# Two attention steps per turn, stages dealt out by turns, and row-wise work by pairs of row tiles, in a graph network with attention

## The chip, the core and the metric

The kernel runs on one core of one Trainium2 chip. The metric is device time in microseconds (us). In the profiles PE is TensorE's matmuls, PEld its weight loads, DVE VectorE, ACT ScalarE, POOL GpSimd, SP the engine that issues DMAs.

## The reference, cut to what matters

Layer 0 is a graph convolution with two batch norms, and the change does not touch it except for the last load. Layer 1, for each of 16 batches of 1024 rows and 256 columns, in four heads of 64:

```python
x = _layernorm(x + layer0(x, ...))
# layer 1
c_adj = mean of each row of x;  diff = c_adj[:, None, :] - c_adj[:, :, None]
Wg = adj * 2*abs(abs(sigmoid(diff) - 0.5) - 0.5)      # 1024 x 1024 per batch, symmetrised
q  = relu(fea @ Wg * para)                             # "graph"
k, v = x @ kv_w
out = softmax(q k^T * scale) v                         # 4 heads
x = _layernorm(x + out)
```

All of it is in fp32.

## The kernel before

For batch b the kernel needs four kinds of work: the attention of b itself; for b+1 the matrix Wg (`wg_a`, `wg_b`), the keys, the values and the queries (`graph`); for b+2 the row-wise work (`bn2`, `ln1_a`, `ln1_b`, `x1_t`, the means and their row `crow`). The finish (division by the softmax's sums, residual, layer norm, store) of b runs partly in b+1. The attention of a batch is cut into 16 steps; a step has 4 fp32 matmuls of scores, 2 exponentials of 128x1024, 2 sums and 4 matmuls of attend. All other work is cut into *pieces*, and a list says in which step each piece is issued:

```python
def put(w, s, f, *a):
    at.setdefault(w * NS + s, []).append((f, a))
# ... for each batch b (cut)
    for j in range(NT):                          # 8 row tiles, one per step
        put(b - 2, 4 + j, bn2, b, j)
        put(b - 2, 5 + j, ln1_a, b, j)
        put(b - 2, 7 + j, ln1_b, b, j)
        put(b - 2, 8 + j, x1_t, b, j)
    put(b - 2, 7 + NT, crow, b)
    # wg: one row tile per step; keys, values: steps 0 to 4; graph: steps 6 to 15 (cut)

for g in ...:
    scores(g + 1); exps(g + 1)                   # one step ahead
    sums(g)
    for f, a in at.get(g, []):
        f(*a)                                    # the pieces of this step
    attend(g)
```

So TensorE issues, per step: scores, pieces, attend. Every other engine gets its instructions in the same order of steps. (In the traces an fp32 matmul shows as two records and a transpose as one, so the four matmuls of scores are `x8`.) The row of means reads its input right behind the work that makes it:

```python
def crow(b):
    nc.vector.tensor_scalar_mul(css[b], css[b], 1.0 / C)     # DVE: the means
    # ... (cut)
    for h in range(NH):
        p = ps_t.tile([P, FB], F32, tag="t", name="pc")
        for k in range(FB // P):                              # TensorE needs them at once
            nc.tensor.transpose(p[:, ts(k, P)], css[b][:, j : j + 1].to_broadcast([P, P]), ident)
        nc.scalar.copy(crows[b][:, ts(h, FB)], p)
```

The matmuls come in forms: scores use 64 rows of the array, two heads side by side; attend uses 64 columns, two heads side by side; the sums of the softmax (`dens`) use 32 columns; everything else uses the full 128x128. In PSUM, the memory that TensorE writes to, stand two tiles of scores (two banks each), one of attend and three for the pieces.

## Time and profile before

| | before |
|---|---|
| time, median of the runs at first | 2781.89 us |
| span of the profile | 2780.6 us |
| period of a batch in the attention | 114.92 us |
| busy per period: PE, DVE, ACT, POOL | 113.7, 73.8, 65.2, 31.4 us |

The table is read thus: PE is busy nearly the whole period, every other engine has over 40 us to spare, so only TensorE's own issue, or something that it waits for, can move the end. The lines for this are in the prediction below. Two more groups, of DVE's row-wise work on one tile of 256 columns (columns: line, engine, operation, tiles, shapes, count; then busy us in total and mean ns of one; then idle time before them and who ended it):

```profile
L564 DVE TENSOR_TENSOR r<-r,x 128x256 f32<-128x256 f32 x128 | 54.4, 425 | 4.4
L557 DVE RECIPROCAL RD<-pf 128x4 f32<-128x4 f32 x128 | 23.1, 180 | 144.4 <-PE pf L555 144.4
```

They are short and many, and none of them makes TensorE wait.

### The profile page before, as it was taken

How to read it: one execution, taken by the hardware profiler on the slowest of the kernel's cores; microseconds unless marked ns; L12 is line 12 of the kernel's file. 1: busy time of each engine (PE TensorE's matmuls, PEld its weight loads, DVE VectorE, ACT ScalarE, POOL GpSimd, SP SyncE). 2: the span in 40 equal slices, each digit the busy share in tenths (PEclk: the TensorE clock that was granted, in tenths of full speed). 3: DMA queues.
4: the chain of work that ended last, by engine and by line, in shares of the span. 5: the costliest groups of instructions: out<-in, count | busy, mean ns of one | idle time of the engine just before them, and what ended most of it. 6: DMA issues, size and time to landing. Idle time of an engine off the chain costs nothing.

```text
span 2780.6 us, 26036 instructions
## 1 busy us (share of the span) xinstructions
PE 2724.5 (98%) x9306; PEld 1145.7 (41%) x9306; DVE 1353.0 (49%) x2377; ACT 1297.7 (47%) x1887; POOL 498.1 (18%) x660
## 2 busy tenths in 40 slices
PE   8999999999999899999999999999999999999998
PEld 4444444444444443443434434344343443444432
DVE  3101111112222655756657566575665756657556
ACT  2111111112655564655646546466465564655534
POOL 0000000000000212313223132231322313323113
PEclk9999999999999899999999999999999999999999
DMA  3212211210772200101101001010010100101000
GB/s 121 82 62 84 91 61 76 91 76 0 252 281 90 74 15 16 42 18 33 35 12 42 23 27 35 14 42 25 23 35 14 42 27 22 34 14 42 10 8 24
DMA packets 109992, 147.01 MB, mean 53 GB/s; under 512 B 10272, under 2 KB 92704, under 8 KB 103712
## 3 DMA queue, kind: packets, MB, share of 16 engines
q1 hardware_dynamic: 109856, 145.27, 15.2%
q8 instruction: 76, 1.25, 0.2%
q14 instruction: 60, 0.49, 0.1%
HBM read 86.52 MB, written 58.72 MB: 52 GB/s over the span
## 4 chain that ended last, share of the span: by engine, by line
PE 97%; DVE 2%; DMA 0%; issue 0%; POOL 0%; ACT 0%; SPq 0%; DVEq 0%; POOLq 0%; ACTq 0%
PE s L494 18%; PE o L524 17%; PE pg L474 16%; PE pa L215 16%; PE po L304 8%; PE ph L228 8%; PE pk L447 4%; PE pv L458 4%; PE pf L554 2%; PE pd L543 1%; PE py L387 1%; PE px L408 1%; PE pc L421 1%; PE pf L555 0%; DVE qT L479 0%
## 5 line engine op out<-in xcount | busy, mean ns | idle before, releaser
L506 ACT ACTIVATE e<-s 128x1024 f32<-128x1024 f32 x512 | 496.4, 1021 | 409.4 <-PE s L494 408.9
L494 PE MATMUL s<-qT,kT 64*128 64x512 f32 x2048 | 508.8, 615 | 0.0
L524 PE MATMUL o<-e,v 128*64 128x512 f32 x2048 | 495.7, 605 | 0.0
L515 DVE TENSOR_TENSOR acc<-acc,e 128x1024 f32<-128x1024 f32 x384 | 467.0, 1216 | 41.9 <-ACT e L506 27.5
L474 PE MATMUL pg<-wg,x 128*128 128x512 f32 x1024 | 477.1, 604 | 0.5 <-ACT x1T L409 0.2
L215 PE MATMUL pa<-AhT,x 128*128 128x512 f32 x1024 | 443.7, 594 | 0.5 <-issue 0.5
L247 DVE BATCH_NORM_STATS2 st<-ph 128x6 f32<-128x512 f32 x128 | 89.5, 699 | 560.1 <-ACT hT L246 560.1
L494 PEld LDWEIGHTS s<-qT,kT 64*128 64x128 f32 x2048 | 176.2, 186 | 327.0 <-issue 244.8
L215 PEld LDWEIGHTS pa<-AhT,x 128*128 128x128 f32 x1024 | 195.1, 191 | 246.3 <-issue 244.3
L474 PEld LDWEIGHTS pg<-wg,x 128*128 128x128 f32 x1024 | 182.2, 190 | 240.6 <-issue 213.4
L439 DVE SCALAR_TENSOR_TENSOR wg<-wg,adj_sb 128x1024 f32<-128x1024 f32 x128 | 156.7, 1225 | 171.9 <-ACT wg L435 169.6
L222 ACT COPY agg<-pa 128x512 f32<-128x512 f32 x64 | 37.5, 585 | 407.4 <-PE pa L215 407.4
L228 PE MATMUL ph<-agg,W1T 128*128 128x512 f32 x512 | 222.2, 592 | 0.0
L524 PEld LDWEIGHTS o<-e,v 128*64 128x64 f32 x2048 | 124.2, 136 | 225.5 <-issue 212.6
L66 POOL TENSOR_SCALAR rs_z<-mv_z 128x1 f32<-128x1 f32 x128 | 52.2, 408 | 900.3 <-DVE mv_z L343 889.3
L66 POOL TENSOR_SCALAR rs_a<-mv_a 128x1 f32<-128x1 f32 x128 | 124.8, 975 | 436.3 <-DVE mv_a L343 436.2
L304 PE MATMUL po<-hL,W2T 128*128 128x512 f32 x384 | 165.0, 592 | 0.0
L68 POOL TENSOR_TENSOR rs_a<-rs_a,mhalf 128x1 f32<-128x1 f32 x128 | 157.9, 1234 | 10.7
L409 ACT COPY x1T<-px 128x256 f32<-128x256 f32 x128 | 47.6, 372 | 240.4 <-PE px L408 240.4
L66 POOL TENSOR_SCALAR rs_bn<-mv_bn 128x1 f32<-128x1 f32 x6 | 1.3, 222 | 884.0 <-DVE mv_bn L104 884.0
L228 PEld LDWEIGHTS ph<-agg,W1T 128*128 128x128 f32 x512 | 97.3, 190 | 122.5 <-issue 122.2
L246 ACT COPY hT<-ph 128x512 f32<-128x512 f32 x128 | 74.9, 585 | 144.9 <-PE ph L228 144.9
(106 smaller groups left out, 2486.0 us busy)
## 6 DMA issues: line engine op xcount, KB each, us to landing
h<-hT SPq DMA_DIRECT2D x24, 1024.0 KB, 3.8
hL<-h SPq DMA_DIRECT2D x24, 1024.0 KB, 6.2
x<-in_x_dram SPq DMA_DIRECT2D x16, 1024.0 KB, 5.3
yT<-y SPq DMA_DIRECT2D x32, 512.0 KB, 3.7
yt<-yT SPq DMA_DIRECT2D x128, 128.0 KB, 2.6
xr<-in_x_dram SPq DMA_DIRECT2D x128, 128.0 KB, 2.3
out_dram<-r SPq DMA_DIRECT2D x128, 128.0 KB, 1.7
A<-in_adj_dram SPq DMA_DIRECT2D x4, 1024.0 KB, 7.9
```

What stands on the lines that cost most here:

```text
L66: nc.gpsimd.tensor_scalar(dst, src, add, None, op0=OP.add)
L68: nc.gpsimd.tensor_tensor(dst, src, mhalf[:, :n], OP.pow)
L215: nc.tensor.matmul(p, xts[b][:, k, ts(c, P)], AhT[:, k, ts(h, FB)], start=(k == 0), stop=(k == NT - 1),)
L228: nc.tensor.matmul(p, W1T[:, k, ts(f, P)], aggT[b][:, k, ts(h, FB)], start=(k == 0), stop=(k == CT - 1),)
L304: nc.tensor.matmul(po[c], W2T[:, k, ts(c, P)], hT[u][:, k, :], start=(k == 0), stop=(k == HT - 1))
L439: nc.vector.scalar_tensor_tensor(t, t, 1.0, adj_sb[:, i, :], op0=OP.add, op1=OP.mult)
L447: nc.tensor.matmul(p, kvw[:, k, ts(c, P)], x1Ts[b][:, k, ts(h, FB)], start=(k == 0), stop=(k == CT - 1))
L474: nc.tensor.matmul(pg[b], x1s[b, k][:, ts(c, P)], wgs[b, k][:, ts(h, FB)], start=(k == 0), stop=(k == NT - 1))
L494: nc.tensor.matmul(t[:, h, :], kTs[b, pair][h * HD : (h + 1) * HD, ts(cb, P)], qTs[b, pair][h * HD : (h + 1) * HD, ts(hf, FB)], start=True ...
L506: nc.scalar.activation(E[g, a], S.pop((g, a)), AF.Exp)
L515: nc.vector.tensor_add(ACC[b, hf, pair], ACC[b, hf, pair], E[g, a])
L524: nc.tensor.matmul(O[b, hf, pair][h * HD : (h + 1) * HD, :], vs[b][:, cb, pair * P + h * HD : pair * P + (h + 1) * HD], E[g, a][:, h, :], ...
```

## The change

The intent: fewer changes of the array's form on TensorE (two steps share one turn: scores, pieces, scores, attend, attend), half as many row-wise instructions (two row tiles at once), the means computed a turn ahead of their use, and within a turn the short pieces spread among the long ones, so that their PSUM tiles are evacuated in time. The core of the diff; most buffers, the loads and the general path are cut, and the comments are added:

```diff
-        def crow(b):
-
+        def means(b):
             nc.vector.tensor_scalar_mul(css[b], css[b], 1.0 / C)
...
-        def finish_a(b, i):
-            hf, k = divmod(i, FB // P)
+        def recips(b, hf):                       # one reciprocal for four row tiles
...
+        def finish_a(b, j):                      # two row tiles: one multiply, one add of 512 columns
...
-        ep = pool("ep", 5)
-        accp = pool("accp", 3)
+        ep = pool("ep", 6)
+        accp = pool("accp", 2)
...
         NS = NT // 2 * NP * NH
+        NC = NS // 2                             # 8 turns of two steps
...
+        WG = (3, 3, 1, 1)                        # wg stages in turns 0 to 3
+        KV = (3, 3, 2)                           # keys and values in turns 0 to 2
+        QG = (6, 6, 6, 7, 7)                     # graph pieces in turns 3 to 7
...
+            put(b - 2, NC - 2, means, b)
+            for h in range(NH):
+                put(b - 2, NC - 1, crow, b, h)
...
+        def arrange(pieces):
+            few = sorted((fa for fa in pieces if fa[0] not in long), key=lambda fa: rank.get(fa[0], 11))
+            many = [fa for fa in pieces if fa[0] in long]      # keys, values, graph
+            n = sum(f in short for f, _ in few)
+            res, k, done = [], 0, 0
+            for f, a in few:
+                res.append((f, a))
+                if f in short and f is not dens:
+                    k += 1
+                    upto = len(many) * k // n
+                    res += many[done:upto]
+                    done = upto
+            return res + many[done:]
...
+            scores(g + 2); exps(g + 2)           # (conditions cut)
+            sums(g)
+            for f, a in now:                     # arranged pieces of the turn
                 f(*a)
-            if 0 <= g < nsteps:
-                attend(g)
+            sums(g + 1)
+            scores(g + 3); exps(g + 3)
+            for k in live:                       # g and g + 1
+                attend(k)
```

In `rank` the functions `bn2` and, last of all, `wg_a` and `wg_b` come after the short pieces.

More of the change, by code (lines that the diff above doesn't have):

```diff
@@ L79, in gnn_norm_attention_kernel @@
     yT_dram = [yT_all[b] for b in range(B)]
-    LDP = 3
+    LDP = 2
     s2 = const.tile([P, CT], F32, name="s2")
@@ L273, in load @@
         def load(b, j):
-            yts[b, j] = ldp.tile([P, CT, P], F32, tag="yt", name=f"yt{b}_{j}")
-            nc.sync.dma_start(yts[b, j], yT_dram[b][:, :, ts(j, P)])
-            xrs[b, j] = ldp.tile([P, C], F32, tag="xr", name=f"xr{b}_{j}")
-            nc.sync.dma_start(xrs[b, j], x[b, ts(j, P), :])
+            yts[b, j] = ldp.tile([P, CT, 2 * P], F32, tag="yt", name=f"yt{b}_{j}")
+            nc.sync.dma_start(yts[b, j], yT_dram[b][:, :, ts(j, 2 * P)])
+            xrs[b, j] = ldp.tile([P, 2, C], F32, tag="xr", name=f"xr{b}_{j}")
+            nc.sync.dma_start(xrs[b, j], x[b, ts(j, 2 * P), :].rearrange("(a p) c -> p a c", p=P))
         with ExitStack() as ph2:
@@ L338, in ln_stats, with ln_apply @@
     def ln_stats(sm, r, name):
-        st = sm.tile([P, 6], F32, tag="st", name=f"st_{name}")
-        nc.vector.bn_stats(st, r)
-        mv = sm.tile([P, 2], F32, tag="mv", name=f"mv_{name}")
-        nc.vector.bn_aggr(mv, st)
-        rs = sm.tile([P, 1], F32, tag="rs", name=f"rs_{name}")
-        rsqrt(rs, mv[:, 1:2], EPS)
+        n = r.shape[1]
+        mv = sm.tile([P, n, 2], F32, tag="mv", name=f"mv_{name}")
+        for a in range(n):
+            st = sm.tile([P, 6], F32, tag="st", bufs=2, name=f"st_{name}_{a}")
+            nc.vector.bn_stats(st, r[:, a, :])
+            nc.vector.bn_aggr(mv[:, a, :], st)
+        rs = sm.tile([P, n], F32, tag="rs", name=f"rs_{name}")
+        rsqrt(rs, mv[:, :, 1], EPS)
         return mv, rs
-    def ln_apply(dst, r, mv, rs):
-        nc.vector.tensor_scalar(dst, r, mv[:, 0:1], rs, op0=OP.subtract, op1=OP.mult)
+    def ln_apply(r, mv, rs):
+        nc.vector.tensor_scalar(r, r, mv[:, 0, 0:1], rs, op0=OP.subtract, op1=OP.mult)
     def fast():
@@ L353, in fast @@
         pool = lambda name, bufs, **k: fx.enter_context(tc.tile_pool(name=name, bufs=bufs, **k))
-        x1p = pool("x1p", 21)
+        x1p = pool("x1p", 11)
         x1Tp = pool("x1Tp", 1)
@@ L358, in fast @@
         kp = pool("kp", 2 * CT)
-        qp = pool("qp", CT + 1)
+        qp = pool("qp", 2 * CT + 1)
         vp = pool("vp", 2)
-        ep = pool("ep", 5)
-        accp = pool("accp", 3)
+        ep = pool("ep", 6)
+        accp = pool("accp", 2)
         otp = pool("otp", 3)
         sm = pool("sm", 6)
-        rp = pool("rp", 4)
+        rp = pool("rp", 2)
         ps_s = pool("ps_s", 2, space=PSUM)
@@ L381, in begin @@
             x1Ts[b] = x1Tp.tile([P, CT, N], F32, tag="x1T", name=f"x1T_{b}")
-            css[b] = sm.tile([P, NT], F32, tag="cs", name=f"cs_{b}")
+            css[b] = sm.tile([P, NT], F32, tag="cs", bufs=2, name=f"cs_{b}")
         def ln1_a(b, j):
-            p = ps_t.tile([P, FB], F32, tag="t", name="py")
-            for c in range(CT):
-                nc.tensor.transpose(p[:, ts(c, P)], yts[b, j][:, c, :], ident)
-            x1s[b, j] = x1p.tile([P, C], F32, tag="x1", name=f"x1_{b}_{j}")
@@ L389, in ln1_a @@
-            nc.vector.tensor_add(x1s[b, j], p[:, :C], xrs[b, j])
+            p = ps_t.tile([P, 2, C], F32, tag="t", name="py")
+            for a in range(2):
+                for c in range(CT):
+                    nc.tensor.transpose(p[:, a, ts(c, P)], yts[b, j][:, c, ts(a, P)], ident)
+            x1s[b, j] = x1p.tile([P, 2, C], F32, tag="x1", name=f"x1_{b}_{j}")
+            nc.vector.tensor_add(x1s[b, j], p, xrs[b, j])
             mvs[b, j] = ln_stats(sm, x1s[b, j], f"a{b}_{j}")
         def ln1_b(b, j):
-            r = x1s[b, j]
@@ L394, in ln1_b @@
             mv, rs = mvs.pop((b, j))
-            nc.vector.scalar_tensor_tensor(
-                r,
-                r,
-                mv[:, 0:1],
-                rs.to_broadcast([P, C]),
-                op0=OP.subtract,
-                op1=OP.mult,
-                accum_out=css[b][:, j : j + 1],
-            )
-        def x1_t(b, j):
-            p = ps_t.tile([P, FB], F32, tag="t", name="px")
-            for c in range(CT):
-                nc.tensor.transpose(p[:, ts(c, P)], x1s[b, j][:, ts(c, P)], ident)
-            nc.scalar.copy(x1Ts[b][:, :, ts(j, P)], p[:, :C].rearrange("p (c n) -> p c n", c=CT))
@@ L411, in crow @@
-        def crow(b):
+            for a in range(2):
+                r = x1s[b, j][:, a, :]
+                nc.vector.scalar_tensor_tensor(
+                    r,
+                    r,
+                    mv[:, a, 0:1],
+                    rs[:, a : a + 1].to_broadcast([P, C]),
+                    op0=OP.subtract,
+                    op1=OP.mult,
+                    accum_out=css[b][:, 2 * j + a : 2 * j + a + 1],
+                )
+        def x1_t(b, j):
+            p = ps_t.tile([P, CT, 2 * P], F32, tag="t", name="px")
+            for a in range(2):
+                for c in range(CT):
+                    nc.tensor.transpose(p[:, c, ts(a, P)], x1s[b, j][:, a, ts(c, P)], ident)
+            nc.scalar.copy(x1Ts[b][:, :, ts(j, 2 * P)], p)
@@ L413, in crow @@
+        def means(b):
             nc.vector.tensor_scalar_mul(css[b], css[b], 1.0 / C)
-            hcs[b] = sm.tile([P, NT], F32, tag="hcs", name=f"hcs_{b}")
+            hcs[b] = sm.tile([P, NT], F32, tag="hcs", bufs=2, name=f"hcs_{b}")
             nc.vector.tensor_scalar_mul(hcs[b], css[b], 0.5)
-            crows[b] = crp.tile([P, N], F32, tag="crow", name=f"crow_{b}")
-            for h in range(NH):
-                p = ps_t.tile([P, FB], F32, tag="t", name="pc")
-                for k in range(FB // P):
-                    j = h * (FB // P) + k
-                    nc.tensor.transpose(p[:, ts(k, P)], css[b][:, j : j + 1].to_broadcast([P, P]), ident)
-                nc.scalar.copy(crows[b][:, ts(h, FB)], p)
+        def crow(b, h):
+            if h == 0:
+                crows[b] = crp.tile([P, N], F32, tag="crow", name=f"crow_{b}")
+            p = ps_t.tile([P, FB], F32, tag="t", name="pc")
+            for k in range(FB // P):
+                j = h * (FB // P) + k
+                nc.tensor.transpose(p[:, ts(k, P)], css[b][:, j : j + 1].to_broadcast([P, P]), ident)
+            nc.scalar.copy(crows[b][:, ts(h, FB)], p)
@@ L471, in graph @@
                 pg[b] = ps_t.tile([P, FB], F32, tag="t", name="pg")
-                if h == 0:
-                    qTs[b, c] = qp.tile([P, N], F32, tag="qT", name=f"qT_{b}_{c}")
+                qTs[b, c, h] = qp.tile([P, FB], F32, tag="qT", name=f"qT_{b}_{c}_{h}")
             nc.tensor.matmul(
-                pg[b], x1s[b, k][:, ts(c, P)], wgs[b, k][:, ts(h, FB)], start=(k == 0), stop=(k == NT - 1)
+                pg[b], x1s[b, k // 2][:, k % 2, ts(c, P)], wgs[b, k][:, ts(h, FB)], start=(k == 0), stop=(k == NT - 1)
             )
             if k == NT - 1:
-                qs = qTs[b, c][:, ts(h, FB)]
+                qs = qTs[b, c, h]
                 nc.vector.tensor_mul(qs, pg[b], para_sb[:, c, ts(h, FB)])
@@ L496, in scores @@
                         kTs[b, pair][h * HD : (h + 1) * HD, ts(cb, P)],
-                        qTs[b, pair][h * HD : (h + 1) * HD, ts(hf, FB)],
+                        qTs[b, pair, hf][h * HD : (h + 1) * HD, :],
                         start=True,
@@ L548, in fast @@
         R = {}
-        def finish_a(b, i):
-            hf, k = divmod(i, FB // P)
-            p = ps_t.tile([P, FB], F32, tag="t", name="pf")
-            for pair in range(NP):
-                nc.tensor.transpose(p[:, ts(pair, P)], OT[b, hf, pair][:, ts(k, P)], ident)
-            nc.tensor.transpose(p[:, C : C + P], DT[b, hf][:, ts(k, P)], ident)
-            rd = RD[:, b * NT + i, :]
-            nc.vector.reciprocal(rd, p[:, C : C + P].rearrange("p (h r) -> p h r", r=32)[:, :, 0])
-            r = rp.tile([P, C], F32, tag="r", name=f"r_{b}_{i}")
+        KB = FB // P
@@ new lines, in recips @@
+        def recips(b, hf):
+            p = ps_t.tile([P, KB, P], F32, tag="t", name="pr")
+            for k in range(KB):
+                nc.tensor.transpose(p[:, k, :], DT[b, hf][:, ts(k, P)], ident)
+            i = b * NT + hf * KB
+            nc.vector.reciprocal(
+                RD[:, i : i + KB, :], p.rearrange("p k (h r) -> p k h r", r=32)[:, :, :, 0]
+            )
+        def finish_a(b, j):
+            hf, k = divmod(2 * j, KB)
+            p = ps_t.tile([P, 2, C], F32, tag="t", name="pf")
+            for a in range(2):
+                for pair in range(NP):
+                    nc.tensor.transpose(p[:, a, ts(pair, P)], OT[b, hf, pair][:, ts(k + a, P)], ident)
+            r = rp.tile([P, 2, C], F32, tag="r", name=f"r_{b}_{j}")
+            rd = RD[:, b * NT + 2 * j : b * NT + 2 * j + 2, :].rearrange("p a h -> p (a h)")
@@ L559, in finish_a @@
             nc.vector.tensor_mul(
-                r.rearrange("p (h d) -> p h d", h=HEADS),
-                p[:, :C].rearrange("p (h d) -> p h d", h=HEADS),
-                rd.unsqueeze(2).to_broadcast([P, HEADS, HD]),
-            )
-            nc.vector.tensor_add(r, r, x1s.pop((b, i)))
-            mv, rs = ln_stats(sm, r, f"z{b}_{i}")
-            nm = sm.tile([P, 1], F32, tag="nm", name=f"nm_{b}_{i}")
-            nc.gpsimd.tensor_scalar(nm, mv[:, 0:1], rs, -1.0, op0=OP.mult, op1=OP.mult)
@@ L568, in finish_a @@
-            R[b, i] = (r, rs, nm)
-        def finish_b(b, i):
-            r, rs, nm = R.pop((b, i))
-            nc.scalar.activation(r, r, AF.Identity, bias=nm, scale=rs)
-            nc.sync.dma_start(out[b, ts(i, P), :], r)
+                r.rearrange("p a (h d) -> p (a h) d", h=HEADS),
+                p.rearrange("p a (h d) -> p (a h) d", h=HEADS),
+                rd.unsqueeze(2).to_broadcast([P, 2 * HEADS, HD]),
+            )
+            nc.vector.tensor_add(r, r, x1s.pop((b, j)))
+            mv, rs = ln_stats(sm, r, f"z{b}_{j}")
@@ new lines, in finish_a, with finish_b @@
+            nm = sm.tile([P, 2], F32, tag="nm", name=f"nm_{b}_{j}")
+            for a in range(2):
+                nc.gpsimd.tensor_scalar(
+                    nm[:, a : a + 1], mv[:, a, 0:1], rs[:, a : a + 1], -1.0, op0=OP.mult, op1=OP.mult
+                )
+            R[b, j] = (r, rs, nm)
+        def finish_b(b, j):
+            r, rs, nm = R.pop((b, j))
+            for a in range(2):
+                nc.scalar.activation(
+                    r[:, a, :], r[:, a, :], AF.Identity, bias=nm[:, a : a + 1], scale=rs[:, a : a + 1]
+                )
+            nc.sync.dma_start(out[b, ts(j, 2 * P), :].rearrange("(a p) c -> p a c", p=P), r)
@@ L603, in fast, with put @@
         NS = NT // 2 * NP * NH
+        NC = NS // 2
         at = {}
-        def put(w, s, f, *a):
-            at.setdefault(w * NS + s, []).append((f, a))
-        for b in range(B):
-            put(b - 2, 4, begin, b)
-            for j in range(NT):
-                if b > 0 or j >= LDP:
-                    put(b - 2, 3 + j, load, b, j)
-                put(b - 2, 4 + j, bn2, b, j)
-                put(b - 2, 5 + j, ln1_a, b, j)
-                put(b - 2, 7 + j, ln1_b, b, j)
-                put(b - 2, 8 + j, x1_t, b, j)
-            put(b - 2, 7 + NT, crow, b)
-            for i in range(NT):
-                put(b - 2, 8 + NT + i, wg_a, b, i)
-                put(b - 2, 8 + NT + i, wg_b, b, i)
-            n = 0
+        def put(w, t, f, *a):
+            at.setdefault(w * NC + t, []).append((f, a))
@@ new lines, in fast @@
+        WG = (3, 3, 1, 1)
+        KV = (3, 3, 2)
+        QG = (6, 6, 6, 7, 7)
+        for b in range(B):
+            for hf in range(NH):
+                t = (hf + 1) * (NC // NH)
+                put(b, t, dens, b, hf)
+                put(b, t + 1, recips, b, hf)
+                for k in range(KB // 2):
+                    put(b, t + 1 + k, finish_a, b, hf * (KB // 2) + k)
+                    put(b, t + 2 + k, finish_b, b, hf * (KB // 2) + k)
+            put(b - 2, 2, begin, b)
+            for j in range(NT // 2):
+                if b > 0 or j >= LDP:
+                    put(b - 2, j, load, b, j)
+                put(b - 2, j + 1, bn2, b, j)
+                put(b - 2, j + 2, ln1_a, b, j)
+                put(b - 2, j + 3, ln1_b, b, j)
+                put(b - 2, j + 4, x1_t, b, j)
+            put(b - 2, NC - 2, means, b)
+            for h in range(NH):
+                put(b - 2, NC - 1, crow, b, h)
+            i = 0
+            for t, n in enumerate(WG):
+                for i in range(i, i + n):
+                    put(b - 1, t, wg_a, b, i)
+                    put(b - 1, t, wg_b, b, i)
+                i += 1
@@ L625, in fast @@
             kv = [(keys, (b, c, h)) for c in range(CT) for h in range(NH)]
             kv += [(values, (b, j)) for j in range(0, NT, 2)]
-            for n, (f, a) in enumerate(kv):
-                put(b - 1, n * 5 // len(kv), f, *a)
-            ng = CT * NH * NT
-            for m in range(ng):
-                put(b - 1, 6 + m * 10 // ng, graph, b, m)
-            for i in range(NT):
-                hf = i // (FB // P)
-                s = (hf + 1) * (NS // NH)
-                if i % (FB // P) == 0:
-                    put(b, s, dens, b, hf)
-                put(b, s + 1 + i % (FB // P), finish_a, b, i)
-                put(b, s + 2 + i % (FB // P) + (b == B - 1 and hf == NH - 1), finish_b, b, i)
@@ L640, in fast @@
-        put(B - 1, NS // NH, range_so_far)
-        put(B - 1, NS + FB // P, range_all)
-        nsteps = B * NS
-        for g in range(min(at), max(max(at), nsteps - 1) + 1):
-            if 0 <= g + 1 < nsteps:
-                scores(g + 1)
-                exps(g + 1)
-            if 0 <= g < nsteps:
-                sums(g)
-            for f, a in at.get(g, []):
-                f(*a)
-            if 0 <= g < nsteps:
-                attend(g)
+            for t, n in enumerate(KV):
+                for _ in range(n):
+                    f, a = kv.pop(0)
+                    put(b - 1, t, f, *a)
@@ new lines, in fast @@
+            m = 0
+            for t, n in enumerate(QG):
+                for m in range(m, m + n):
+                    put(b - 1, NC - len(QG) + t, graph, b, m)
+                m += 1
+        put(B - 1, 4, range_so_far)
+        put(B - 1, NC + 2, range_all)
+        nsteps = B * NS
+        order = (dens, recips, finish_a, finish_b, x1_t, ln1_a, ln1_b, means, bn2, load, crow)
+        rank = {f: k for k, f in enumerate(order)}
+        short = (dens, recips, finish_a, x1_t, ln1_a, crow)
+        long = (keys, values, graph)
@@ new lines, in fast @@
+        for t in range(min(at), max(max(at), nsteps // 2 - 1) + 1):
+            g = 2 * t
+            now = arrange(at.get(t, []))
+            live = [k for k in (g, g + 1) if 0 <= k < nsteps]
+            ahead = [k for k in (g + 2, g + 3) if 0 <= k < nsteps]
+            if ahead:
+                scores(g + 2)
+                exps(g + 2)
+            while now and now[0][0] is dens:
+                f, a = now.pop(0)
+                f(*a)
+            if live:
+                sums(g)
+            if not now and live:
+                attend(g)
+                live.pop(0)
+                sums(g + 1)
+            for f, a in now:
+                f(*a)
+            if now and live:
+                sums(g + 1)
+            if ahead:
+                scores(g + 3)
+                exps(g + 3)
+            for k in live:
+                attend(k)
@@ L687, in general @@
             nc.vector.tensor_add(r, p[:, :C], r)
-            ln_apply(r, r, *ln_stats(sm, r, f"g{j}"))
+            ln_apply(r, *ln_stats(sm, r.unsqueeze(1), f"g{j}"))
             nc.vector.tensor_reduce(cs[:, j : j + 1], r, AX.X, OP.add)
@@ L763, in general @@
                 )
-            ln_apply(r, r, *ln_stats(sm, r, f"gz{i}"))
+            ln_apply(r, *ln_stats(sm, r.unsqueeze(1), f"gz{i}"))
             nc.sync.dma_start(out[bass.ds(b, 1), ts(i, P), :].rearrange("o p c -> p (o c)"), r)
```

## The prediction

> **What bounds the kernel now.** I read the page first, its engine table and the chain that ended last:
>
> ```profile
> PE 2724.5 (98%) x9306; PEld 1145.7 (41%) x9306; DVE 1353.0 (49%) x2377; ACT 1297.7 (47%) x1887; POOL 498.1 (18%) x660
> ...
> PE 97%; DVE 2%; DMA 0%; issue 0%; POOL 0%; ACT 0%; SPq 0%; DVEq 0%; POOLq 0%; ACTq 0%
> ```
>
> TensorE is the bound from end to end; no other engine is busy half the time. So a microsecond is won only if TensorE issues its work in fewer slots or waits less. Layer 0 (to about 910 us) isn't touched by the change. The attention repeats: the chain shows the first keys group of a batch at 1559.48, 1674.40 and 1789.33. The busy time by stretch over two such batches (columns: stretch, its length, then busy us of PE, PEld, DVE, ACT, POOL, then clock, DMA share, GB/s):
>
> ```profile
> 1559.48:1674.40 114.92, 113.72 (x450) 46.36 (x449) 73.78 (x130) 65.18 (x93) 31.36 (x40) 1.00 0.09 28
> 1674.40:1789.33 114.93, 113.73 (x450) 46.36 (x449) 73.78 (x130) 65.19 (x93) 31.36 (x40) 1.00 0.09 28
> ```
>
> A batch takes 114.92 us at full clock, equal to 0.01 us: a period set by one engine. ACT has 50 us of slack per batch and DVE 41.
>
> Next the TensorE timeline, where the difference of two starts is what a group costs. First two steps of a batch, then the start and the end of the attention:
>
> ```profile
> 1800.59 1.94 PE L524 MATMUL o<-e,v 128*64 128x512 f32 x8
> 1802.45 1.99 PE L494 MATMUL s<-qT,kT 64*128 64x512 f32 x8
> 1804.37 0.44 PE L554 MATMUL pf<-ident,ot 128*128 128x128 f32 x2
> 1804.65 0.27 PE L555 MATMUL pf<-ident,dt 128*128 128x128 f32 x1
> 1804.76 1.89 PE L458 MATMUL pv<-kvw,x1T 128*128 128x256 f32 x8
> 1806.58 1.94 PE L524 MATMUL o<-e,v 128*64 128x512 f32 x8
> ...
> 1810.75 3.62 PE L458 MATMUL pv<-kvw,x1T 128*128 128x256 f32 x16
> 1814.30 1.94 PE L524 MATMUL o<-e,v 128*64 128x512 f32 x8
> ```
>
> ```profile
> 976.56 0.38 PE L408 MATMUL px<-ident,x 128*128 128x128 f32 x2
> 976.87 1.99 PE L494 MATMUL s<-qT,kT 64*128 64x512 f32 x8
> 978.79 1.12 PE L474 MATMUL pg<-wg,x 128*128 128x512 f32 x2
> ...
> 2760.53 3.65 PE L524 MATMUL o<-e,v 128*64 128x512 f32 x16
> 2764.11 1.07 PE L543 MATMUL pd<-acc,ones 128*32 128x512 f32 x8
> ```
>
> A scores group costs 1.92 us and an attend group 1.86. Sixteen pv records cost 3.55 and eight 1.82, so one costs 0.216 and eight without the switch 1.73: leaving full-array work for a tiled form costs 0.09. A graph group shows the entry: eight records after scores take 3.54 us (1828.23 to 1831.77), six take 2.68 (1835.86 to 1838.54); one is 0.43, six are 2.58, so entering costs 0.10. Two attends in a row cost 3.58, not 2 x 1.86 = 3.72.
>
> One true wait stands in the list of groups, once per prepared batch, where the transposes for the row of means wait for DVE:
>
> ```profile
> L421 PE MATMUL pc<-ident,cs 128*128 128x128 f32 x128 | 17.8, 284 | 18.0 <-DVE cs L413 18.0
> ```
>
> 18.0 us over 15 batches is 1.2 each.
>
> **What the Trainium skill says.** "Trainium Kernel Development and Optimization", Performance Expectations, calls matmul busy time a bad measure of the distance to the roofline, as matmuls are pipelined. The trace agrees: PE is 98% busy, yet the switches above lie within busy time. "TensorE: Matmul & The Clock Gate", Part 3, The mechanism, says matmuls in different tiles of the array overlap. It agrees: eight s records of half the rows take 1.92 us, four slots of 0.43 and a surcharge of 0.2. The surcharges come from this trace alone. "Perfetto Trace Analysis", Tensor Engine Instruction, says that ACT, DVE and GpSimd are strict FIFO. The ACT timeline agrees: the pv group above ends at 1806.65, its copy starts after the activation queued ahead of it:
>
> ```profile
> 1805.94 1.14 ACT L434 ACTIVATE wg<-crow,cs 128x1024 f32<-128x1024 f32 x1
> 1807.12 1.06 ACT L435 ACTIVATE wg<-wg 128x1024 f32<-128x1024 f32 x1
> 1808.08 0.57 ACT L465 COPY v<-pv 128x512 f32<-128x512 f32 x1
> ```
>
> **The change part by part.**
> (1) Two steps per turn. Before, two steps are twice scores, pieces, attend: 2 x (1.92 + 0.10 entry + 0.09 exit + 1.86) = 7.94 us beside the pieces. After, a turn is scores, pieces, scores, attend, attend: 1.92 + 0.10 + 0.09 + 1.92 + 3.58 = 7.61. (That scores cost 1.92 after full-array work too is the line at 976.87.) 0.33 saved per turn, 8 turns a batch: 2.6 us.
> (2) Means one turn before the row transposes: the 1.2 us wait goes.
> (3) Pairs of row tiles. The transposes on TensorE stay as many (64 per batch); only their evacuations merge. DVE: a 256-wide operation is 0.425 us, a 512-wide one 0.69 (the qT multiply), so a pair saves 0.16 on three operations, 64 times each: 31 us; the reciprocals (23.1 us) go from 128 to 32. The bn2 activations go from 256 of 0.486 to 128 of about 0.60 (the size of r), 35 us less ACT. POOL's powers and adds halve. All of it lies beside TensorE and moves the end by nothing, except in the tail: after the last attend DVE works through four row tiles one by one until 2773.2; in pairs it saves some 1.5 us.
> (4) Buffers: s keeps two tiles, e gets six, acc two, PSUM three for pieces. In a turn the second exps need e tiles that attend frees; I find that this fits where ACT and DVE are on time.
> Sum of gains: 2.6 + 1.2 = 3.8 per batch, 57 us over 15 batches, and 1.5: about 2723.
>
> (5) What is given back. Pieces are sorted: short ones first with the long between, and after them bn2 and the wg stages. I walked ACT's queue through each turn with the durations above. The wg stages are dealt 3, 3, 1, 1 over turns 0 to 3. In **turn 1** the queue is: first exps, the copies of one keys and two values pieces, two bn2 (1.2), three wg stages (odd 1.15, even 1.15 + 1.06, odd 1.15: 4.5), and only then the second exps. The second values copy can't start before the last TensorE piece is done. Count from the start of the second scores: copy done at 0.7, bn2 1.9, wg 6.4, first exp (1.02) 7.4. TensorE finishes scores and two attends at 1.92 + 3.58 = 5.5 and then needs the first s tile, which that exp frees at about 7.5. **A new wait of 2.0 us** on ACT, once per batch. Turn 0 escapes: its wg stages stand ahead of the key copies and run beside the TensorE pieces (exp done near 12.1 us of a 13.7 us turn).
> In turn 1 DVE also gets its last wg stage late (it ends about 8.5 us after the second scores began), then two sums of 1.2: they end 3.4 us into turn 2. Behind them in DVE's queue stand one more sum and the evacuation of the first finish transposes, to about 5.4 us; the fourth PSUM tile of turn 2 is wanted at about 4.6. **Another wait of about 0.9**. Turns 3 to 7 come out without one. So about 2.9 us are given back per batch, 14 times in full, about 1.7 in the batch whose turn 1 has no bn2: 42 us.
>
> Net: 57 + 1.5 - 42 = 16 us. The start of the attention stays latency-bound in both; pairs halve the operations, two loads ahead in place of three make it wait more; I count zero, give or take 3. 2781.9 - 16 = 2766; I say **2764**.
>
> **The rivals.** A: no new wait, if ACT's wg work hides somehow (a different order in the queue, or shorter work). For it: ACT is busy only 65 of 115 us, and the turns were evidently dealt out by hand. Against: strict order, and 7.4 us of queue against 5.5 of cover. Then 2723, faster by 2.1%. B: only the ACT wait appears, as DVE catches up or the tile allocator gives a free PSUM tile: 2750. C: waits grow in further turns (late sums hold e tiles, exps slip, scores wait again; loads for pairs of 256 KB arrive late with two buffers): 4 us or more per batch, 2780 or beyond. DVE as the bound is out: 74 us of work in 111. A DMA bound is out: its share is 0.09.
>
> **Range and chances.** I give my walk the most weight, A about one in six, C about one in eight. Range 2720 to 2781. The 2% line is at 2726.3; only A crosses it: faster 0.16, same 0.82, slower 0.02.
>
> **What would show it.** Right in (1): attend groups of 16 records at 3.58 us, scores groups twice around the pieces, no pc wait on DVE. Right in (5): in the list of waits, TensorE's s loads wait for ACT e (or the wg ahead of it), some 2 us, about 15 times, in the second turn of each batch, and pv waiting near 0.9 us on DVE r in the turn after; the period of a batch about 113.9 us. Wrong: a period near 111.1 with no wait (A), or waits in most turns (C), or an attention that begins later than 977 us by over 3.

## The result, and the profile after

The changed kernel takes 2754.66 us (median of 4 runs, 2753.3 to 2755.14) against 2781.87 of before in the same rounds. The ratio is 0.9902, 95% interval 0.9885 to 0.9919: 1.0% faster, within 2%. Ratios here are the mean time of one kernel's fast runs over that of the other's fast runs of the same rounds, so not quite the ratio of the medians quoted.

The page of the changed kernel, engine table and chain:

```profile
PE 2684.0 (98%) x9306; PEld 1153.1 (42%) x9306; DVE 1305.4 (47%) x2089; ACT 1249.2 (45%) x1695; POOL 184.4 (7%) x404
...
PE 90%; DVE 5%; ACT 3%; issue 1%; DMA 0%; POOL 0%; SPq 0%; DVEq 0%; ACTq 0%; POOLq 0%
```

TensorE has the same 9306 matmul records as before and is still the bound, but the chain that ended last now runs through DVE and ACT for 8% of the span, where it was 2%. One period, from the first keys of a batch to those of the next (columns as in the prediction):

```profile
2343.97:2457.01 113.04, 111.26 (x450) 46.66 (x449) 70.84 (x112) 62.18 (x81) 10.27 (x24) 1.00 0.09 28
```

The period fell from 114.92 to 113.04 us, and 1.8 us of it is now time in which PE is idle (1.2 before, the wait for the means). TensorE's timeline from the end of turn 1 of a batch into turn 2 shows where; in brackets stands the idle time before the group and who ended it:

```profile
1571.63 1.99 PE L500 MATMUL s<-qT,kT 64*128 64x512 f32 x8
1573.55 3.65 PE L530 MATMUL o<-e,v 128*64 128x512 f32 x16
1578.48 2.04 PE L500 MATMUL s<-qT,kT 64*128 64x512 f32 x8 [1.27 <-ACT e L512]
1580.45 0.66 PE L571 MATMUL pf<-ident,ot 128*128 128x128 f32 x4
1580.94 1.89 PE L465 MATMUL pv<-kvw,x1T 128*128 128x256 f32 x8
1582.67 0.60 PE L390 MATMUL py<-ident,yt 128*128 128x128 f32 x4
1583.78 0.92 PE L465 MATMUL pv<-kvw,x1T 128*128 128x256 f32 x3 [0.51 <-DVE r L574]
```

The joined attends are there (16 records). Scores and attends end at 1571.63 + 1.92 + 3.58 = 1577.13, and the next scores start at 1578.48: a wait of 1.35. The second values piece starts 1.11 after the py transposes where four transposes take 0.44: a wait of 0.67. Each is followed by a slower restart (the scores group after it takes 1.97 in place of 1.92, the values group 1.92 in place of 1.82), so that the two cost 1.35 + 0.05 + 0.67 + 0.10 = 2.2 us per batch. No other group of the period waits. ACT's timeline in the same stretch:

```profile
1571.74 0.58 ACT L472 COPY v<-pv 128x512 f32<-128x512 f32 x1 [1.14 <-PE pv L465]
1572.22 1.09 ACT L380 ACTIVATE yt<-yt,t,s 128x256 f32<-128x256 f32 x2
1573.21 1.14 ACT L437 ACTIVATE wg<-crow,hcs 128x1024 f32<-128x1024 f32 x1
1574.25 1.14 ACT L441 ACTIVATE wg<-crow,cs 128x1024 f32<-128x1024 f32 x1
1575.42 1.06 ACT L442 ACTIVATE wg<-wg 128x1024 f32<-128x1024 f32 x1
1576.38 1.13 ACT L437 ACTIVATE wg<-crow,hcs 128x1024 f32<-128x1024 f32 x1
1577.42 1.92 ACT L512 ACTIVATE e<-s 128x1024 f32<-128x1024 f32 x2
```

From the last values copy to the exponentials ACT has no gap: it is a queue, two bn2 and three wg stages long, and the scores tile that TensorE wants comes free only when the first of the two exponentials is done. Note the starts: an instruction of 1.14 us is followed after 1.04, except where the next one reads its result (L442 follows L441 after 1.17).

The groups of DVE that were shown before are now half or a quarter as many, and wider:

```profile
L579 DVE TENSOR_TENSOR r<-r,x 128x512 f32<-128x512 f32 x64 | 44.3, 692 | 2.2
L562 DVE RECIPROCAL RD<-pr 128x16 f32<-128x16 f32 x32 | 8.2, 257 | 68.8 <-PE pr L560 68.7
```

POOL fell from 498.1 to 184.4 us busy, DVE from 1353.0 to 1305.4, ACT from 1297.7 to 1249.2.

Where the 27.9 us of span (2780.6 to 2752.7) went, by the starts of groups in both traces:

| stretch | before | after | difference |
|---|---|---|---|
| start to the first keys of batch 2 | 1099.81 | 1100.60 | +0.8 |
| 13 periods, to the first keys of batch 15 | 1493.95 | 1469.44 | -24.5 |
| from there to the end of the last attend | 170.35 | 165.18 | -5.2 |
| tail, to the end | 16.5 | 17.5 | +1.0 |

### The profile page after: what moved, and what is told of

Its sections match the earlier page's. It is cut to its first block, busy times and chain, and to the rows that moved or that the text cites. A ratio compares the mean times of both kernels' runs of the same rounds, so it can differ in the third digit from the quotient of the medians.

```text
span 2752.7 us, 24565 instructions
## 1 busy us (share of the span) xinstructions
PE 2684.0 (98%) x9306; PEld 1153.1 (42%) x9306; DVE 1305.4 (47%) x2089; ACT 1249.2 (45%) x1695; POOL 184.4 (7%) x404
## 4 chain that ended last, share of the span: by engine, by line
PE 90%; DVE 5%; ACT 3%; issue 1%; DMA 0%; POOL 0%; SPq 0%; DVEq 0%; ACTq 0%; POOLq 0%
PE pa L215 16%; PE s L500 16%; PE pg L480 16%; PE o L530 15%; PE po L304 8%; PE ph L228 8%; PE pk L454 4%; PE pv L465 3%; DVE wg L446 1%; PE px L413 1%; PE pd L549 1%; PE py L390 1%; PE pf L571 1%; DVE acc L521 1%; PE pr L560 1%
## 5 line engine op out<-in xcount | busy, mean ns | idle before, releaser
L480 PE MATMUL pg<-wg,x 128*128 128x512 f32 x1024 | 470.4, 593 | 0.6 <-DVE wg L446 0.6
L530 PE MATMUL o<-e,v 128*64 128x512 f32 x2048 | 467.7, 599 | 0.0
L530 PEld LDWEIGHTS o<-e,v 128*64 128x64 f32 x2048 | 135.6, 136 | 316.4 <-issue 315.3
L222 ACT COPY agg<-pa 128x512 f32<-128x512 f32 x64 | 37.4, 585 | 404.7 <-PE pa L215 404.7
L518 DVE TENSOR_TENSOR acc<-e,e 128x1024 f32<-128x1024 f32 x64 | 78.2, 1221 | 153.1 <-PE pd L549 153.1
L485 DVE TENSOR_TENSOR qT<-pg,para_sb 128x512 f32<-128x512 f32 x64 | 44.2, 690 | 204.3 <-PE pg L480 204.3
L465 PE MATMUL pv<-kvw,x1T 128*128 128x256 f32 x512 | 119.4, 382 | 6.6 <-DVE r L574 6.6
L308 DVE BATCH_NORM_STATS2 st<-po 128x6 f32<-128x512 f32 x64 | 44.7, 698 | 169.4 <-PE po L304 169.4
L454 PE MATMUL pk<-x1T,kvw 128*128 128x512 f32 x256 | 117.3, 601 | 1.0 <-ACT kT L457 1.0
```

Source lines behind the costliest of these rows:

```text
L454: nc.tensor.matmul(p, kvw[:, k, ts(c, P)], x1Ts[b][:, k, ts(h, FB)], start=(k == 0), stop=(k == CT - 1))
L465: nc.tensor.matmul(p[:, ts(a, C)], x1Ts[b][:, k, ts(j + a, P)], kvw[:, k, C:], start=(k == 0), stop=(k == CT - 1),)
L480: nc.tensor.matmul(pg[b], x1s[b, k // 2][:, k % 2, ts(c, P)], wgs[b, k][:, ts(h, FB)], start=(k == 0), stop=(k == NT - 1))
L530: nc.tensor.matmul(O[b, hf, pair][h * HD : (h + 1) * HD, :], vs[b][:, cb, pair * P + h * HD : pair * P + (h + 1) * HD], E[g, a][:, h, :], ...
```

## The experiments

The theory is that of the prediction: the change saves 2.6 us per batch by fewer changes of form and 1.2 by the earlier means, and gives back two waits (1.35 and 0.67 as measured), one on ACT's queue and one on DVE's. The rivals: that too few e tiles make the exponentials late, that the gain comes from the pairs, or that the means' wait only moves. Four kernels ran on one chip, three on another, each timed in three rounds against the kernel before (2782.29 and 2782.36 us there). One more was planned, a seventh e tile: the pools then no longer fit into the on-chip memory, and the kernel does not build.

| kernel | time, us | ratio to before | period, us |
|---|---|---|---|
| before | 2781.87 | 1 | 114.92 |
| after | 2754.66 | 0.9902 (0.9885 to 0.9919) | 113.04 |
| act_first | 2722.64 | 0.9783 (0.9767 to 0.9800) | 110.86 |
| wg_even | 2746.05 | 0.9871 (0.9854 to 0.9887) | 112.37 |
| dve_halves | 2755.32 | 0.9901 (0.9885 to 0.9918) | 113.16 |
| one_step | 2769.90 | 0.9956 (0.9940 to 0.9973) | 113.85 |
| mul_first | 2745.59 | 0.9872 (0.9856 to 0.9889) | 112.26 |
| act_sums | 2721.08 | 0.9780 (0.9764 to 0.9796) | 110.86 |
| means_early | 2765.40 | 0.9938 (0.9922 to 0.9955) | 113.78 |

All gave correct results.

### act_first: ACT's own work ahead of the last long pieces

```diff
+            shorts = sum(f in short and f is not dens for f, _ in few)
...
                     k += 1
+                    if k == shorts:
+                        continue
                     upto = len(many) * k // n
```

After the last short piece no long ones are inserted, so bn2 and wg are issued before the remaining keys, values and graph pieces. In turn 1 the order on TensorE stays what it was, as bn2 and wg have nothing there.

> Edit: in a turn, the pieces that follow the last short one (bn2, wg) are queued ahead of the remaining keys, values and graph pieces; TensorE's own order does not change. Theory (ACT's queue: the wg work of turn 1 stands behind the last values copy): both waits go, the scores wait of turn 1 (1.35 us a batch) and the pv wait of turn 2 (0.67), as the late wg causes both; period 113.0 to 111.1, time about 2727. Rival (e tiles too few, so the second exps of a turn start late whatever the queue holds): waits stay, 2755. Second rival (the two waits have separate causes): only the first goes, about 2736.

Measured: 2722.64 us, 32 us less than the changed kernel, and a period of 110.86 us in which PE is busy throughout (columns of the first line as in the prediction). Then ACT in turn 1:

```profile
2205.99:2316.85 110.86, 110.86 (x449) 46.67 (x449) 70.85 (x112) 62.15 (x81) 13.98 (x24) 1.00 0.09 29
```

```profile
2331.96 0.58 ACT L457 COPY kT<-pk 128x512 f32<-128x512 f32 x1 [1.22 <-PE pk L454]
2332.44 1.09 ACT L380 ACTIVATE yt<-yt,t,s 128x256 f32<-128x256 f32 x2
...
2336.60 1.13 ACT L437 ACTIVATE wg<-crow,hcs 128x1024 f32<-128x1024 f32 x1
2337.64 1.05 ACT L472 COPY v<-pv 128x512 f32<-128x512 f32 x2
2338.79 1.94 ACT L512 ACTIVATE e<-s 128x1024 f32<-128x1024 f32 x2
```

bn2 and the wg stages now follow the key copy instead of the last values copy, while TensorE is still at its pieces, and the two values copies come after them. The second scores of this turn begin at 2335.74, so the exponentials start 3.05 us after them, in place of 5.79, and no scores wait. Group by group TensorE's period is the same as in the changed kernel, to 0.01 us, but for the two waits and the two restarts behind them: 2.18 us, 28 us over 13 periods; another 3.2 us lie before the first keys of batch 2. So this order brings what the prediction's rival A ("a different order in the queue") put at 2723. The rival with too few e tiles falls: their number is unchanged and both waits are gone. That both went does not show that one causes the other; the next two runs bear on this.

### wg_even: the wg stages dealt evenly

```diff
-        WG = (3, 3, 1, 1)
+        WG = (2, 2, 2, 2)
```

> Edit: wg stages dealt 2, 2, 2, 2 over turns 0 to 3 in place of 3, 3, 1, 1. Theory: in turn 1 one odd wg stage of 1.05 us less behind the last copy, so the scores wait falls from 1.35 to about 0.3 us; turn 2 gets one more and may wait about 0.2; the pv wait of turn 2 shrinks below 0.2. Period about 111.7, time about 2736. Rival (e tiles): no change, 2755.

Measured: 2746.05 us, period 112.37. The second part of the expectation failed. TensorE in the same two turns:

```profile
2360.97 2.05 PE L500 MATMUL s<-qT,kT 64*128 64x512 f32 x8 [0.24 <-ACT e L512]
...
2366.28 0.92 PE L465 MATMUL pv<-kvw,x1T 128*128 128x256 f32 x3 [0.51 <-DVE r L574]
```

By the slots the scores wait fell from 1.35 to 0.31, as expected, but the values wait of turn 2 stayed at 0.67. The reason can be read from the traces: as long as scores wait for ACT at all, turn 2 begins one exponential after the last wg of ACT, and DVE's chain (the last wg's two operations and three sums) also begins at that last wg. Dealing the stages otherwise moves both, and the distance between them stays: from the first scores of turn 2 to the evacuation behind the sums it is 4.56 us in the changed kernel and 4.58 here.

### mul_first: the finish evacuation ahead of a sum on DVE

```diff
-            while now and now[0][0] is dens:
+            while now and now[0][0] in (dens, finish_a):
```

> Edit on the changed kernel: in turns 2 and 6 the finish piece is queued ahead of the first sum, so its evacuation on DVE comes 1.2 us earlier; nothing else moves. Theory (the pv wait of turn 2 is DVE's queue, separate from ACT's, which makes the scores wait): pv wait 0.67 to 0, scores wait still 1.35, period 112.4, time about 2745. Rival (the pv wait follows from ACT's late queue, or from the copies): no change, 2755.

Measured: 2745.59 us, period 112.26, where 112.4 was expected; the restart of 0.10 behind the wait went with it. The same places on TensorE:

```profile
2361.53 2.04 PE L500 MATMUL s<-qT,kT 64*128 64x512 f32 x8 [1.28 <-ACT e L512]
...
2366.16 1.03 PE L465 MATMUL pv<-kvw,x1T 128*128 128x256 f32 x4
```

The values wait is gone, the scores wait is untouched. So the two waits stand in two queues, ACT's and DVE's, and each can be removed alone; act_first removed both because it brings DVE's last wg stage earlier relative to the turn: it starts 3.34 us before the first scores of turn 2, where in the changed kernel it starts 0.83 before them.

### one_step: two steps per turn undone

```diff
-            for f, a in now:
-                f(*a)
-            if now and live:
-                sums(g + 1)
+            for f, a in now[:cut]:               # half of the turn's pieces, by TensorE's time
+                f(*a)
+            attend(live.pop(0))                  # (condition cut)
             scores(g + 3); exps(g + 3)
+            sums(g + 1)
+            for f, a in now[cut:]:
+                f(*a)
             for k in live:
                 attend(k)
```

> Edit: of the change, two steps per turn is undone: each step has scores, its half of the turn's pieces, and its own attend; the rest (pairs, means a turn earlier, deal of the stages) stays. Theory: 0.33 us more a turn in switches of the array's form, 2.6 a batch, 39 in all, and the waits of turns 1 and 2 change with the cover, by minus 2 to plus 1 a batch: 2765 to 2800, attend groups back at 1.86 us. Rival (the gain is from pairs or the means alone): 2755 or less.

Measured: 2769.90 us, period 113.85. The period, and the only group that waits within it (in the list, attend's 3.1 us over 13 batches):

```profile
2354.45:2468.30 113.85, 113.61 (x450) 45.44 (x449) 70.70 (x112) 61.91 (x81) 20.64 (x24) 1.00 0.09 28
L530 PE MATMUL o<-e,v 128*64 128x512 f32 x2048 | 495.4, 605 | 3.1 <-ACT ot L540 3.1
```

Neither of the two waits is in this trace. Attend waits 0.31 per batch for ACT's copy of its PSUM tile (by the slots between values and attend, 0.62 in place of 0.31 once a batch). Without that the period is 113.54, against 110.86 of act_first, which has two steps per turn and no wait either: **2.68 us per batch for the changes of form**, where the prediction's sum said 2.6. By the starts of groups 1.21 of it lie in the attends (16 groups of 1.87 us against 8 of 3.58) and 1.47 in the pieces, which TensorE enters and leaves 16 times in a batch here and 8 times there; the scores take 30.7 us in both.

### means_early: of the change only the earlier means, on the kernel before

```diff
-            put(b - 2, 7 + NT, crow, b)
+            put(b - 2, 6 + NT, means, b)
+            put(b - 2, 7 + NT, crow, b)
```

(`means` is the DVE part cut out of `crow`.)

> Edit on the kernel before: of the whole change only the means, which are computed one step ahead of the transposes of their row. Theory: the wait of the pc transposes on DVE (18.0 us over 15 batches by the list, 1.36 a batch by the slots) goes, the rest stays: period 114.92 to 113.6, time 2762 to 2764. Rival (the wait only moves to the next transposes or to the row's copy): 2780 to 2782.

Measured: 2765.40 us and a period of 113.78, 1.14 us less than before. The time is 1.4 us above the expected range. On TensorE (an attend closes the step):

```profile
2571.29 1.28 PE L423 MATMUL pc<-ident,cs 128*128 128x128 f32 x8
2572.49 1.94 PE L526 MATMUL o<-e,v 128*64 128x512 f32 x8
```

The means' transposes start 0.22 us after the px pair in front of them (2571.07), which is that pair's own time (0.11 each), so the wait for DVE, 1.36 by the slots, is gone. But the group takes 1.20 where it took 0.99: in front of its fifth transpose 0.24 us have come, in which the weight load waits for ACT's copy of px (the trace's releaser, 15 times). So the rival came true for a small part, and 1.36 - 0.24 is about the 1.14 measured. In the whole change the two halves of these transposes stand apart, with graph pieces between, and each takes 0.44 without a wait: there the full 1.36 is gained. Alone, this edit brings 17 us, where the whole change brought 27.

### dve_halves: the pair-wide DVE operations undone

```diff
-            nc.vector.tensor_add(x1s[b, j], p, xrs[b, j])
+            for a in range(2):
+                nc.vector.tensor_add(x1s[b, j][:, a, :], p[:, a, :], xrs[b, j][:, a, :])
```

and likewise for the multiply and the residual add of the finish.

> Edit: the three pair-wide DVE operations (x1 add, product with the reciprocals, residual add) undone into halves of 256, 192 operations more, some 31 us of DVE busy time. Theory (off the path, save that the first finish evacuation of turn 2 is in the pv wait): end moves by 0.1 to 0.2 us a batch, 2755 to 2758. Rival (the pairs are part of the gain): the time rises by 10 us or more, 2765.

Measured: 2755.32 us, against 2754.66 of the changed kernel (different rounds; the ratios to before are 0.9901 and 0.9902). The end does not move beyond the noise, so the pairs on DVE are no part of the gain (those on ACT and POOL were not undone). What was not expected is the cost: DVE is busy not 31 us more but 4 us less (1301.1 us), since two halves that do not depend on each other overlap. The timeline of DVE, two halves each:

```profile
1583.96 0.75 DVE L576 TENSOR_TENSOR r<-pf,RD 128x256 f32<-128x256 f32 x2
1584.63 0.75 DVE L582 TENSOR_TENSOR r<-r,x 128x256 f32<-128x256 f32 x2
```

From their start to that of the next instruction two halves take 0.67 us (1583.96 to 1584.63). A wide operation whose result the next one reads takes 0.69 and a gap of 0.03, so 0.72; two of 256 columns in such a chain, as before the change, 2 x (0.425 + 0.03) = 0.92.

### act_sums: act_first, and both sums ahead of the pieces

```diff
             if live:
                 sums(g)
+                sums(g + 1)
...
-            if now and live:
-                sums(g + 1)
```

> Edit on the kernel with ACT's work first: both sums of a turn queued ahead of its pieces. Theory (no wait is left within a batch, period 110.86; the last turn's sums come earlier on DVE so that the last pd does not wait): period unchanged, end earlier by 1 to 2 us in the tail, 2721. Rival (sums in front delay the evacuations in turns with finish pieces, whose first PSUM tiles TensorE wants back): waits of 0.5 us or more in turns 1, 2 or 5, period above 111.3, 2730 or more.

Measured: 2721.08 us, period 110.86, no wait within a batch. In the changed kernel the last softmax sums on TensorE wait for DVE; here they do not. First the changed kernel, then this one:

```profile
2736.92 1.05 PE L549 MATMUL pd<-acc,ones 128*32 128x512 f32 x4 [0.65 <-DVE acc L521]
```

```profile
2702.49 1.22 PE L549 MATMUL pd<-acc,ones 128*32 128x512 f32 x8
```

The tail from the first of the last eight pd matmuls to the end is 17.5 us there, 17.8 in act_first and 15.6 here (16.5 before the change). This is the fastest version run, 2.2% below the kernel before and 1.2% below the changed one. Against act_first it was timed only through the kernel before, on another chip, so the 1.6 us between the two are indicated by the tail (up to the last flag matmul, which waits for DVE, it is 1.5 us shorter) and not shown by a direct comparison.

## Why the prediction was right, and where it was off

The measured time lies in the range and in the class that was forecast; it lies 9.3 us below the number given, so the gain of 27 us was more than the 18 that were forecast. The range, 61 us wide, took in the rivals A and B too, and B's 2750 is nearer to the measured time than the 2764; it is the traces that bear out the mechanism. The number itself is 2 us below the prediction's own sum of 2766, for no stated reason.

1. *What bounds the kernel.* Right: TensorE stayed the bound, and a shorter period is the whole gain.
2. *Two steps per turn, 2.6 us per batch.* Right: 2.68 between one_step, less its own wait, and act_first. Joined attends take 3.58 us in the trace. One term is not general: entering costs 0.10 for keys, values and graph, but 0.05 for transposes (four take 0.49 after scores, 0.44 after other pieces).
3. *Means a turn earlier, 1.2 us.* Right, and a little small: 1.36 by the slots, of which means_early alone got 1.14. With the 2.68 that makes 4.04 of the 4.06 us between before and act_first.
4. *Pairs lie beside TensorE and move nothing but the tail.* Right in the steady state (dve_halves for DVE; for ACT and POOL only 0.02 us of the period is left unexplained). ACT fell by 48.5 us, not 35: the merged copies of x1_t (47.6 to 37.4) were not counted, and bn2 fell further (111.8 to 69.7). The tail went the other way, +1.0 in place of -1.5. DVE's part of it, from the first reciprocal to the last statistics, did fall, from 7.05 to 5.75 us, but it began 2.0 us later: the last sums had moved behind the pieces, which the prediction overlooked, and TensorE waits for them.
5. *A new wait on ACT in turn 1, 2.0 us, and one on DVE in turn 2, 0.9.* Both came, in those turns and on those engines: 1.35 and 0.67, and 2.18 with the restarts behind them. **The mis-sized term is this one.** The ACT queue was summed by the durations of its instructions, 7.4 us with the first exponential; by the starts of the trace it took 1577.42 - 1571.63 = 5.79 and the exponential 1.02, so 6.81. Each of its instructions starts some 0.1 us before the one in front of it has ended, but for the one that reads the result of its predecessor. In the 13 full periods the gain was 24.5 us, where the prediction's terms (3.8 - 2.9 each) give 11.7; of these 12.8 more, 0.7 x 13 = 9.4 are the smaller waits, and most of the rest is the 1.36 of the means.
6. *The cause of the DVE wait.* The prediction tied it to the late wg of turn 1. It holds that DVE's queue makes it (mul_first), but a wg stage less in turn 1 does not shorten it (wg_even), since turn 2 moves with it as long as scores wait for ACT.
7. *The start of the attention, zero give or take 3.* The stretch up to batch 2 is 0.8 us longer, and the first scores come at 977.32 us in place of 976.87; the latency of the first row tiles was not tested further.
8. *The last two batches.* They gained 5.2 us. The prediction has no figure for them; by its terms (2.6 for the forms in each, 1.7 given back in the first) it would be 3.5 at most. This was not looked into further.

The page "ScalarE: Activation LUTs" of the Trainium skill, in the section What ACT_TABLE_LOAD costs, has the sentence that would have sized the wait: "Back-to-back ACTIVATEs overlap by ≈ 93 ns." The trace agrees where the second does not read what the first writes: 1.14 us long, 1.04 apart. The page "TensorEngine Tiling (Array Packing)", Key Properties, says that a change of the tiling mode drains TensorE, and gives no figure; the trace shows 0.09 us where full-array work is followed by a tiled form, 0.10 on entering full-array matmuls (0.05 if they are transposes) and some 0.2 of surcharge in a scores group. That these are that drain is inferred.

Open: what made the last two batches gain more than a period does, and whether more e tiles would do anything.

## What to carry to other kernels

When TensorE is the bound, count the changes of the array's form in the order of its instructions, and then walk the other engines' queues through one period: a queue that runs in order can delay the one instruction that frees TensorE's next buffer, however idle that engine is on average. Work of an engine that depends on nothing recent belongs in its queue ahead of the copies that wait for the bound engine, not behind them. Take the length of a queue from the distances of starts, not from durations, and ask of each instruction whether it reads what the one in front of it writes.

## What the Trainium skill lacked or had wrong

- "TensorEngine Tiling (Array Packing)", Key Properties, says that a mode switch drains the engine but has no cost. Here: leaving full-array work 0.09 us, entering full-array matmuls 0.10 (transposes 0.05), scores groups 1.92 us for four slots of 0.43; joining two steps is worth 0.33 us per turn by the sum, and 2.68 us per batch of eight turns by the runs.
- "VectorE: DVE Perf Modes", The TRN2 errata, says that many small tiles pay the fixed latency each time. It does not tell instructions that depend on each other from others. Here two dependent ones of 256 columns take 0.92 us and one of 512 takes 0.72 before an instruction that reads its result, but two independent ones of 256 take 0.67, so the saving is had without the wider instruction.
- "ScalarE: Activation LUTs", What ACT_TABLE_LOAD costs, gives the overlap of 93 ns without exception. Here it is 0.09 to 0.10 us between independent instructions, but one that reads the result of the one before (L442 behind L441) starts 0.03 us after its end.
- "Perfetto Trace Analysis", Tensor Engine Instruction, says that ACT and DVE are strict FIFO. Against bubbles that such an engine causes while it is not saturated, the page advises to break up instructions; it has nothing on their order in the queue, which cost most here: an engine 45% busy made the bound engine wait 1.35 us per batch, and a different order removed it (32 us in all, with the wait on DVE and the start).
